# Two-layer graph attention on one core: x1 of layer 0 turned by DMA transposes of its 16-bit halves instead of by TensorE

## The chip, the cores and the metric

The kernel runs on one core of a Trainium2 chip. A core has TensorE (PE, matrix products and transposes through PSUM), VectorE (DVE), ScalarE (ACT), GpSimd (POOL) and SyncE (SP), whose queue issues every DMA of this kernel. The metric is the device time of one execution in microseconds, as a median over runs: 2969.35 before the change (3 runs, 2967.16 to 2970.29).

## The reference

`x` is 128 graphs of 64 nodes with 768 features, in f32; `adj` is a 0/1 matrix of each graph. Two layers follow each other, each with a residual and a layernorm. Cut to what is computed:

```python
# layer 0: additive graph attention, 12 heads of 64, a gate, residual, layernorm
h = einsum('bnd,ade->bane', x, W); th = tanh(h)
attn = th @ w_src + swap(th @ w_dst)              # one term of the row node, one of the column node
attn = where(attn >= 0, attn, 0.2 * attn)
attn = softmax(where(adj, attn, -999.0))
f = elu(einsum('banm,bame->bane', attn, h) + b)   # heads side by side
gate = sigmoid(x @ H_w.T + H_b)
x = layernorm(x + gate * f + (1 - gate) * x)      # the kernel's x1
# layer 1: scaled dot-product attention, 6 heads of 128, mask adj
q, k, v = heads(x @ Wq + bq), heads(x @ Wk + bk), heads(x @ Wv + bv)
ctx = softmax(q @ k.T / sqrt(128) + where(adj, 0, -9e15)) @ v
x = layernorm(x + ctx @ Wf + bf)
```

## The kernel before

**Tiles.** The 8192 nodes are 64 tiles of 128 rows (two graphs each), taken as 32 pairs of 256 rows (`PAIR`, `NP` = 32). A product of a pair with a 768x768 weight is cut into 2x2 blocks and done with seven block products instead of eight, by the scheme of Strassen and Winograd: sums of blocks of the data (`block_sums`, L184) and of the weight (`weight_sums`, L165) come first, and the results are added together on the way out of PSUM. A `Job` (L200 to L250) is one such product, and `step(job, i)` (L257) issues block product i (three matmuls of f32, which show as six in the trace) and then the way out of the step before it. The jobs have letters: `h` is x times W, `g` the gate, `v` the values of layer 1, `q` and `k` its queries and keys. Capital letters, and `u`, are jobs of a neighbouring turn: `H` is the `h` of the next pair, `u` the `v` that the turn before began.

**Turns.** Layer 0, with the `v` product of layer 1, is one loop of 33 turns (L875 to L978). Turn p computes `h` and the gate of pair p (its tiles are called n0 and n1) and finishes attention, elu, gate, residual and layernorm of pair q = p - 1 (tiles t0 and t1), turns its x1 and begins its `v`. The order of the block products in a turn is written out by hand: `FIRST` (turn 0), `SECOND` (turn 1), `TURN` without its first two steps (turn 2), `TURN` (turns 3 to 31), and `LAST` (turn 32, in which queries and keys of layer 1 begin). All other work hangs on positions in that list: `was(pos, ...)` for the old pair, `at(pos, ...)` for the new one. The actions of a position are emitted behind its block product, in each engine's own queue, which runs strictly in that order. Tables such as `LAST_AT` send a position elsewhere in some turns.

**What a turn of the old pair does.** `probs_by_nodes` transposes the probabilities, `attend` multiplies them with h, `features` divides by the sums and takes the exponential, `elu1` and `gated` make x1, `stats` and `normed` its layernorm (ScalarE writes x1, SP stores it to `x1_d` for layer 1's residual). `by_features` (L814) then brings a tile of x1 into the layout with features on partitions: two times three 128x128 transposes on TensorE into PSUM (`transposed`, L734), each three copied by ScalarE into `x1T`, which holds the pair. `x1T` is stored to `x1T_d` for queries and keys (`spill_features`), and is the data of the `v` job. `value_sums` (L855) allots four tiles `sv` and prepares their sums on VectorE.

**What it does for the new pair.** `products` (L656) takes tanh of h and multiplies it by both attention vectors, one on VectorE, one on GpSimd; `terms` (L665) sums per head into `sd`, stores the column term to DRAM (`dstd`) and loads it back broadcast to all rows (`dd`, two transfers); `with_bias` adds the bias to h and swaps halves of it through two transfers (`hx`); `logits`, `leaky`, `masked`, `exps` make the unnormalized probabilities. `x_sums` makes the block sums of the next pair's x on GpSimd.

**Queues.** Each `dma_start` is on SP, which executes them in the order of emission, and an instruction that waits holds all behind it. A tile of a pool with `bufs=1` (`x1T`, `sv`) can be written again only after its last reader.

The positions of the old code around the turning of x1:

```python
was(8, do(by_features, t1), do(stats, t0))
was(9, do(normed, t0))
was(12, do(v_begins))
was(15, lambda: v_sums[q][0](), lambda: v_sums[q][1](), do(spill_features, q))
was(16, lambda: v_sums[q][2]())
was(19, lambda: v_sums[q][3]())
...
was(11, do(by_features, t0))
```

Of the kernel before, what the change touches and what calls it, by code (L numbers as in the profile page):

```python
# [8 lines left out]

F32 = mybir.dt.float32  # L10
U8 = mybir.dt.uint8
AF = mybir.ActivationFunctionType
ALU = mybir.AluOpType
AX = mybir.AxisListType

P = 128
N = 64
D = 768
KC = D // P
HK = KC // 2  # L20
HALF = D // 2
H0, E0 = 12, 64
J0 = H0 // 2
EP = E0 + 2
H1, E1 = 6, 128
# [5 lines left out]
PAIR = 2  # L31
# [10 lines left out]
B11, B21, B22, T1, T2, T3, T4 = range(7)  # L42
# [21 lines left out]


LAST = [
    "u4", "u3", "q1", "q2", "k1", "k2", "q6", "q5", "q7", "Q1", "q4", "Q2", "q3", "k6", "k5", "k7",
    "Q6", "k4", "k3", "v1", "v2", "v6", "v5", "v7", "K1", "v4", "v3",
]
LAST_REST = [(1, 2), (0, 5), (1, 6), (0, 7), (1, 5), (1, 7), (0, 4), (0, 3), (1, 4), (1, 3)]  # L70
LAST_AT = {3: 3, 4: 4, 5: 6, 6: 8, 7: 9, 8: 11, 9: 12, 11: 15, 12: 16, 15: 20, 16: 20, 19: 22}

ENDS = [
    (0, 1), (0, 2), (0, 6), (0, 5), (0, 7), (1, 1), (0, 4), (0, 3), (1, 6), (1, 5),
    (1, 7), (1, 2), (1, 3), (1, 4),
]
TURN = [
    "h1", "h2", "u4", "u3", "h6", "g1", "h5", "h7", "g2", "g6", "h4",
    "h3", "g5", "g7", "v1", "v2", "g4", "v6", "g3", "v5", "v7",
]  # L80

THIRD_AT = {pos: max(pos - 2, 0) for pos in range(len(TURN))}
TURNS = {
    0: (FIRST, FIRST_AT, {}),
    1: (SECOND, SECOND_AT, SECOND_OLD),
    2: (TURN[2:], THIRD_AT, THIRD_AT),
}


# [1 line left out]
def kernel(  # L91
# [21 lines left out]
    nc = tc.nc  # L113
    NP = x.shape[0]
# [15 lines left out]

    x1_d = [dram.tile([P, PAIR, D], F32, name=f"x1d_{p}") for p in range(NP)]
    x1T_d = [dram.tile([P, KC, PAIR * P], F32, name=f"x1Td_{p}") for p in range(NP)]
    v_d = [dram.tile([P, D], F32, name=f"vd_{t}") for t in range(2 * NP)]
    dst_d = [dram.tile([P, H0], F32, name=f"dstd_{t}") for t in range(2 * NP)]

# [38 lines left out]
    def all_of(steps):  # L174
        for s in steps:
            s()

    def sum_tiles(pool, tag, n, name):
        return [
            pool.tile([P, HK, n], F32, tag=f"{tag}{i}", name=f"{tag}{i}_{name}", bufs=1)  # L180
            for i in range(1, 5)
        ]
# [345 lines left out]
    with ExitStack() as ph, ExitStack() as ph_r:  # L528
# [18 lines left out]
                ts.append(t)  # L547
            return ts

        def sums_of(eng, pool, tag, t, name):  # L550
            return block_sums(
                eng,
                sum_tiles(pool, tag, P, name),
                t[:, :HK, :P],
                t[:, HK:, :P],
                t[:, :HK, P:],
                t[:, HK:, P:],
            )
# [14 lines left out]
        wsd = sbr.tile([P, 2, D], F32, name="wsd", bufs=1)  # L573
        nc.sync.dma_start(out=wsd[:, 0, :], in_=wdst.partition_broadcast(P))
        nc.sync.dma_start(out=wsd[:, 1, :], in_=wsrc.partition_broadcast(P))
        A[0], x_steps = sums_of(G, sbr, "sx", xTs[0], "x0")
        all_of(x_steps)
        t1, t2, t4, t3 = weight_sums(V, w0_w)
        all_of((t1, t2, t3, t4))
# [2 lines left out]
        def work(name):  # L582
            return sb.tile([P, D], F32, tag="work", name=name, bufs=5)
# [59 lines left out]
        def v_job(p):  # L643
# [9 lines left out]
                lambda b: S.copy(at(1, 0), b),  # L653
            )

        def products(t):  # L656

            h = st[t]["h"]
            th = sbr.tile([P, 2, D], F32, tag="th", name=f"th_{t}")
            S.activation(th[:, 1, :].rearrange("p (a e) -> p a e", e=E0), h[:, :, :E0], AF.Tanh)  # L660
            V.tensor_tensor(th[:, 0, :], th[:, 1, :], wsd[:, 0, :], ALU.mult)  # L661
            G.tensor_tensor(th[:, 1, :], th[:, 1, :], wsd[:, 1, :], ALU.mult)  # L662
            st[t]["th"] = th

        def terms(t):  # L665

            th = st[t].pop("th")
            sd = small.tile([P, 2 * H0], F32, tag="sd", name=f"sd_{t}")
            V.tensor_reduce(sd, th.rearrange("p s (a e) -> p (s a) e", e=E0), AX.X, ALU.add)
            st[t]["sd"] = sd  # L670
            nc.sync.dma_start(out=dst_d[t], in_=sd[:, :H0])
            dd = work(f"dd_{t}")
            for g in range(2):
                nc.sync.dma_start(
                    out=dd[g * N : (g + 1) * N, :],
                    in_=dst_d[t][g * N : (g + 1) * N, :]
                    .rearrange("m a -> (m a)")
                    .partition_broadcast(N),
                )
            st[t]["dd"] = dd  # L680
# [128 lines left out]
            next(st[t].pop("norm"), None)  # L809
            nc.sync.dma_start(out=x1_d[t // 2][:, t % 2, :], in_=st[t]["x1"])  # L810

        x1Ts, B = {}, {}

        def by_features(t):  # L814
            p, i = divmod(t, 2)
            if p not in x1Ts:
                x1Ts[p] = sb.tile([P, KC, PAIR * P], F32, tag="x1T", name=f"x1T_{p}", bufs=1)
            x1 = st[t].pop("x1")
            for half in range(2):
                transposed(  # L820
                    x1Ts[p][:, 3 * half : 3 * half + 3, i * P : (i + 1) * P],
                    x1[:, half * HALF : (half + 1) * HALF],
                    f"x1Tp_{t}_{half}",
                )

        def spill_features(p):
            nc.sync.dma_start(out=x1T_d[p], in_=x1Ts[p])
# [25 lines left out]
                nc.sync.dma_start(out=v_d[t], in_=st[t].pop("v"))  # L853

        def value_sums(q):  # L855
            B[q], v_sums[q] = sums_of(V, sb, "sv", x1Ts[q], f"v{q}")

        def x_sums(p):
            operands, steps = sums_of(G, sbr, "sx", xTs[p], f"x{p}")
            all_of(steps)  # L860
            A.setdefault(p, {}).update(operands)

        def third_begins():
            x = xTs[2]
            A[2] = {1: x[:, :HK, :P], 2: x[:, HK:, :P]}
            jobs["H"] = h_job(2)

        row_sums = []

# [10 lines left out]
        for p in range(NP + 1):  # L880
# [2 lines left out]
            t0, t1, n0, n1 = 2 * q, 2 * q + 1, 2 * p, 2 * p + 1  # L883
            if new:
                jobs["G"] = jobs.get("g")
                jobs["h"], jobs["g"] = jobs["H"] if p == 2 else h_job(p), gate_job(p)
            plan = {}

            turn, of_new, of_old = TURNS.get(p, (TURN, {}, {})) if new else (LAST, {}, LAST_AT)

            def at(pos, ok, *acts, places=of_new):
                if ok:
                    plan.setdefault(places.get(pos, pos), []).extend(acts)

            def was(pos, *acts):
                at(pos, old, *acts, places=of_old)

            def do(f, *args):
                return lambda: f(*args)
# [6 lines left out]
            was(0, do(probs_by_nodes, t1))  # L906
            at(0, old, do(exps, t0), do(gate_tanh, t1), places={0: 6} if p == 1 else of_old)
            was(1, do(residual, t1))
            was(2, do(attend, t1), do(gate_tanh, t0))
            was(3, do(features, t1), do(probs_by_nodes, t0), do(residual, t0))  # L910
            was(4, do(elu1, t1), do(gated, t1))
            was(5, do(attend, t0), do(stats, t1))
            was(6, do(features, t0), do(normed, t1))
            was(7, do(elu1, t0), do(gated, t0))
            was(8, do(by_features, t1), do(stats, t0))
            was(9, do(normed, t0))
            was(12, do(v_begins))
            was(15, lambda: v_sums[q][0](), lambda: v_sums[q][1](), do(spill_features, q))
            was(16, lambda: v_sums[q][2]())
            was(19, lambda: v_sums[q][3]())  # L920

            at(0, p + 1 < NP, do(load_xT, p + 1))
            at(3, new, lambda: adjs.__setitem__(p, load_adj(sb, 2 * p, PAIR, f"adj_{p}")))
            at(6, new, do(mask, p))
            at(4, 0 <= p - 2 < NP, do(spill_values, p - 2))
            at(8, new, do(inputs, p))
            at(11, new, do(products, n1))
            was(11, do(by_features, t0))
            at(12, new, do(products, n0))
            at(13, new, do(terms, n1), do(with_bias, n1))  # L930
            at(14, new, do(terms, n0), do(with_bias, n0))
            at(15, new, do(plus_one, p))
            at(16, new, do(logits, n1))
            at(17, new, do(leaky, n1))
            at(17, p + 1 < NP, do(x_sums, p + 1), places={17: 12} if p == 0 else of_new)
            at(18, new, do(masked, n1), do(logits, n0))
            at(19, new, do(exps, n1), do(leaky, n0))
            at(20, new, do(masked, n0))

            if p == NP - 1:  # L940

                q_sums = weight_sums(G, w0_w)[:2] + weight_sums(V, w0_w)[2:]
                k_sums = weight_sums(G, hw_w)
                for pos, block in ((2, B11), (3, B21), (8, T3), (15, B22)):
                    at(pos, True, do(load_block, wq, w0_w, block))
                for pos, block in ((6, B11), (9, B21), (19, T3), (19, B22)):
                    at(pos, True, do(load_block, wk, hw_w, block))
                at(16, True, q_sums[0])
                at(18, True, queries_begin, q_sums[1])
                at(19, True, lambda: all_of(row_sums[:2]))  # L950
            if p == NP:
                flush()
                for act in plan.pop(0):
                    act()
                for pos, act in zip((1, 2, 2, 3, 4, 5, 7, 9), row_sums[2:] + q_sums[2:] + k_sums):
                    plan.setdefault(pos, []).append(act)
# [4 lines left out]
                    at(8, True, do(load_block, wv, wv_w, block))  # L961
                at(7, True, lambda: V.tensor_scalar(b01_bc, b01_bc, 1.0, None, ALU.add))
            if p == 1:
                at(14, True, third_begins, places={})
                for pos, act in zip((4, 5, 7, 8), weight_sums(V, wv_w)):
                    at(pos, True, act, places={})
            for pos, acts in carried.items():
# [119 lines left out]
```

## Time and profile before

| what | us |
|---|---|
| median of 3 runs | 2969.35 |
| the profiled execution | 2970.77 |
| its span, first to last instruction | 2969.0 |
| TensorE busy within the span | 2925.2 |
| matmuls that transpose x1 (x1Tp, 384) | 52.6 |
| matmuls that transpose probabilities (pTp, 384) | 57.6 |
| ScalarE copies x1T out of PSUM (128) | 55.0 |
| mean granted TensorE clock | 0.995 |

Median time from issue to landing, and the size of one transfer: `dd<-dstd` 192 KB, 3.4 us; `x1d<-x` 384 KB, 2.6 us; `vd<-v` 384 KB, 2.9 us; `hx<-h` 99 KB, 3.1 us; `dstd<-sd` 6 KB, 1.9 us; `x1Td<-x1T` 768 KB, 4.8 us.

How to read it: busy time of a group is the union of its instructions, so matmuls that overlap are counted once, while the mean duration of one is longer. A timeline line has the start, the time to the end of the last of the merged instructions, the engine (SPq is SP's queue of DMA issues), the line of the kernel, the operation, what it writes and reads, how many were merged, and in brackets the idle time of the engine before it with what ended it. A line of windows has the stretch, its length, then the busy time and the number of instructions of PE, weight loads, DVE, ACT and POOL, the granted clock, the share of the DMA engines and GB/s.

### The profile page before, as it was taken

Reading aid. Unit: us, or ns where it says so; the run is one execution under the profiler, and the core shown is the slowest. Engines: PE = TensorE matmul, PEld = TensorE weight load, DVE = VectorE, ACT = ScalarE, POOL = GpSimd, SP = SyncE. Lnnn points to the kernel's source line nnn. Section 1 sums busy time; section 2 is a strip of 40 time slices with the busy share of each in tenths; the row PEclk is TensorE's granted clock in tenths of the full one; section 3 lists DMA queues with packets and bytes.
Section 4 is the critical chain, followed back from the end, with each engine's and each line's share of the span. In section 5 each row is a group of like instructions: output and inputs, shape, how many; then the busy total and the mean of one; then the engine's idle time right before and its main releaser. Section 6 shows DMA issues by size and latency. Waiting matters only on the chain.

```text
span 2969.0 us, 45314 instructions
## 1 busy us (share of the span) xinstructions
PE 2925.2 (99%) x18048; PEld 2023.0 (68%) x18048; DVE 1796.9 (61%) x3017; ACT 1009.0 (34%) x1761; POOL 811.1 (27%) x650
## 2 busy tenths in 40 slices
PE   7999999999999999999999999999999999999999
PEld 4566666666666666666578777787777887777875
DVE  6878888788788878887844344333343443443345
ACT  2344344444443444444422222222222222222221
POOL 2434333333343333333422212211111212121121
PEclk9999999999999999999999999999999999999999
DMA  5333333334333333343532211222212222112221
GB/s 171 122 109 114 107 121 115 103 118 128 104 119 104 121 113 106 115 129 103 176 97 77 70 60 55 86 86 76 68 52 64 86 76 73 59 57 82 87 80 48
DMA packets 179681, 284.81 MB, mean 96 GB/s; under 512 B 46736, under 2 KB 113296, under 8 KB 179472
## 3 DMA queue, kind: packets, MB, share of 16 engines
q1 hardware_dynamic: 179472, 281.93, 29.1%
q8 instruction: 143, 2.34, 0.3%
q14 instruction: 66, 0.54, 0.1%
HBM read 167.81 MB, written 101.06 MB: 91 GB/s over the span
## 4 chain that ended last, share of the span: by engine, by line
PE 94%; DVE 3%; DMA 1%; ACT 1%; issue 0%; SPq 0%; POOLq 0%; POOL 0%; DVEq 0%; ACTq 0%
PE y_k L222 8%; PE y_o L222 8%; PE y_q L222 8%; PE y_v L222 8%; PE y_h L222 8%; PE y_g L222 8%; PE z_v L222 4%; PE z_o L222 4%; PE z_k L222 4%; PE z_h L222 4%; PE z_q L222 4%; PE z_g L222 4%; PE x_k L222 2%; PE x_o L222 2%; PE x_q L222 2%; PE x_h L222 2%
## 5 line engine op out<-in xcount | busy, mean ns | idle before, releaser
L789 POOL TENSOR_TENSOR x<-gate,x 128x768 f32<-128x768 f32 x64 | 117.4, 1835 | 323.8 <-ACT gate L840 309.0
L457 POOL TENSOR_TENSOR y<-y,bf_bc 128x768 f32<-128x768 f32 x64 | 115.3, 1832 | 311.4 <-DMA y<-x1d 311.4
L481 DVE TENSOR_TENSOR y<-y_o,y 128x384 f32<-128x384 f32 x128 | 71.4, 557 | 202.1 <-PE y_o L222 198.0
L339 DVE TENSOR_TENSOR kT<-z_k,kT 128x256 f32<-128x256 f32 x96 | 40.8, 425 | 239.3 <-PE z_k L222 136.1
L662 POOL TENSOR_TENSOR th<-th,wsd 128x768 f32<-128x768 f32 x64 | 117.2, 1832 | 182.5 <-DVE th L661 182.5
L274 POOL TENSOR_TENSOR rs_b<-ve_b,minus_half 128x1 f32<-128x1 f32 x64 | 35.1, 548 | 452.5 <-DVE ve_b L272 451.7
L192 POOL TENSOR_TENSOR sq_q<-a,a 128x768 f32<-128x768 f32 x16 | 29.2, 1828 | 432.8 <-PE y_o L222 286.9
L222 PE MATMUL y_h<-w_wq,xT 128*128 128x384 f32 x384 | 136.3, 492 | 8.6 <-DMA w_wq<-in_w_dram 7.9
L222 PE MATMUL y_k<-a,hw_wk 128*128 128x256 f32 x576 | 144.6, 387 | 0.0
L222 PE MATMUL y_q<-a,w_wq 128*128 128x256 f32 x576 | 140.9, 381 | 1.9 <-ACT qT L338 1.9
L222 PE MATMUL z_v<-wv,sv_v 128*128 128x384 f32 x384 | 138.9, 498 | 3.2 <-DVE v L652 3.2
L222 PE MATMUL y_q<-sq_q,w_wq 128*128 128x256 f32 x576 | 140.3, 380 | 0.9 <-ACT qT L338 0.9
L222 PE MATMUL y_h<-w_wq,sx_x 128*128 128x384 f32 x384 | 136.5, 492 | 4.2 <-ACT h L622 4.2
L222 PE MATMUL z_q<-sq_q,w_wq 128*128 128x256 f32 x576 | 140.1, 379 | 0.0
L222 PE MATMUL y_k<-sq_q,hw_wk 128*128 128x256 f32 x576 | 140.1, 379 | 0.0
L222 PE MATMUL z_k<-sq_q,hw_wk 128*128 128x256 f32 x576 | 140.0, 379 | 0.0
L338 ACT ACTIVATE qT<-y_q,bq_c 128x256 f32<-128x256 f32 x144 | 67.4, 469 | 213.2 <-PE y_q L222 213.2
L222 PE MATMUL y_v<-wv,sv_v 128*128 128x384 f32 x384 | 136.6, 492 | 3.0 <-DVE sv_v L193 3.0
L386 ACT ACTIVATE sc<-sc 128x512 f32<-128x512 f32 x48 | 30.2, 630 | 319.3 <-DVE sc L385 319.3
L222 PE MATMUL z_h<-w_wq,sx_x 128*128 128x384 f32 x384 | 137.6, 495 | 0.9 <-DVE w_wq L168 0.9
L222 PE MATMUL y_g<-hw_wk,sx_x 128*128 128x384 f32 x384 | 134.9, 488 | 2.4 <-DVE hw_wk L171 2.2
L222 PE MATMUL y_v<-wv,x1T 128*128 128x384 f32 x384 | 136.1, 491 | 1.2 <-ACT x1T L739 1.0
(171 smaller groups left out, 6678.1 us busy)
## 6 DMA issues: line engine op xcount, KB each, us to landing
x<-in_x_dram SPq DMA_DIRECT2D x64, 384.0 KB, 3.6
dd<-dstd SPq DMA_DIRECT2D x128, 192.0 KB, 3.4
x1d<-x SPq DMA_DIRECT2D x64, 384.0 KB, 2.6
x1Td<-x1T SPq DMA_DIRECT2D x32, 768.0 KB, 4.8
vd<-v SPq DMA_DIRECT2D x64, 384.0 KB, 2.9
a<-x1Td SPq DMA_DIRECT2D x64, 384.0 KB, 3.6
v<-vd SPq DMA_DIRECT2D x384, 64.0 KB, 2.3
y<-x1d SPq DMA_DIRECT2D x64, 384.0 KB, 4.1
```

The costliest lines, as they stand in the source:

```text
L192: lambda: e.tensor_tensor(s1, a21, a22, ALU.add),
L222: T.matmul(to[:, : self.n], lhsT, rhs, start=kc == 0 and not more, stop=kc == HK - 1, skip_group_check=more,)
L274: G.tensor_tensor(rstd, ve, minus_half, ALU.pow)
L338: lambda mn, bk_: S.activation(at(*mn), bk_, AF.Identity, bias=bias(mn[1])),
L339: lambda mn, bk_: V.tensor_tensor(at(*mn), bk_, at(*mn), ALU.add),
L386: S.activation(sc, sc, AF.Exp, scale=SCALE)
L457: G.tensor_tensor(y, y, pools["bf"], ALU.add)
L481: V.tensor_tensor(at(*mn), b, at(*mn), ALU.add)
L662: G.tensor_tensor(th[:, 1, :], th[:, 1, :], wsd[:, 1, :], ALU.mult)
L789: G.tensor_tensor(xp, st[t]["gate"], xp, ALU.mult)
```

## The change

For the pairs q = 2 to 30, `by_features` is no longer called. `apart` splits each word of x1 into its upper and lower 16 bits with strided copies: on ScalarE, and for one half of the odd tile on GpSimd. `send` stores the two halves of a tile as separate rows to a new DRAM buffer `halves_d`. `turned` issues six DMA transposes of two-byte elements for the pair, [512 rows, 128 columns] each, from DRAM into the memory of `sv`. `joined` puts the halves together as words of `x1T` with four strided ScalarE copies. The pairs 0, 1 and 31 (`by_pe`) keep the TensorE transposes.

The steps of a turn are re-ordered: `v` now begins with its products 1 and 2 in the last two positions of the turn, and its other five (`u6 u5 u7 u4 u3`) run in the next turn; the first two products of the next pair's `h` are done a turn earlier (`H1 H2`) from turn 2 on. `sv` is one tile for both uses, `tanh` and `spread` are split from `products` and `terms`, the sums of x are made in two parts, and the tables of positions are new.

```diff
 LAST = [
-    "u4", "u3", "q1", "q2", "k1", "k2", "q6", "q5", "q7", "Q1", "q4", "Q2", "q3", "k6", "k5", "k7",
-    "Q6", "k4", "k3", "v1", "v2", "v6", "v5", "v7", "K1", "v4", "v3",
+    "u6", "u5", "q1", "u7", "q2", "u4", "k1", "u3", "k2", "q6", "q5", "q7", "Q1", "q4", "Q2", "q3", "k6",
+    "k5", "k7", "Q6", "k4", "k3", "v1", "v2", "v6", "v5", "v7", "K1", "v4", "v3",
 ]
...
 TURN = [
-    "h1", "h2", "u4", "u3", "h6", "g1", "h5", "h7", "g2", "g6", "h4",
-    "h3", "g5", "g7", "v1", "v2", "g4", "v6", "g3", "v5", "v7",
+    "h6", "u6", "h5", "u5", "h7", "u7", "g1", "h4", "u4", "g2", "h3",
+    "u3", "g6", "g5", "g7", "H1", "H2", "g4", "g3", "v1", "v2",
 ]
 
-THIRD_AT = {pos: max(pos - 2, 0) for pos in range(len(TURN))}
+TURN_AT = {11: 8, 12: 13, 13: 12, 14: 14, 16: 15, 17: 16, 18: 17, 19: 18}
+THIRD = [
+    "h6", "u4", "h5", "u3", "h7", "g1", "h4", "g2", "h3", "g6", "g5", "g7",
+    "H1", "H2", "g4", "g3", "v1", "v2",
+]
...
+NO_NEXT = [
+    "h6", "u6", "h5", "u5", "h7", "u7", "g1", "h4", "g2", "u3", "h3",
+    "g6", "g5", "g7", "u4", "g4", "g3", "v1", "v2",
+]
...
+        def apart(t):
+
+            sp = work(f"sp_{t}").bitcast(U16).rearrange("p (two e) -> p two e", two=2)
+            x1 = words(st[t].pop("x1"))
+            if t % 2:
+                G.tensor_copy(sp[:, 0], x1[:, 0])
+            else:
+                S.copy(sp[:, 0], x1[:, 0])
+            S.copy(sp[:, 1], x1[:, 1])
+            st[t]["halves"] = sp
+
+        def send(t):
+            p, i = divmod(t, 2)
+            nc.sync.dma_start(
+                out=halves_d[p][:, i * P : (i + 1) * P, :].rearrange("h t d -> t h d"),
+                in_=st[t].pop("halves"),
+            )
+
+        def turned(p):
+
+            sv[p] = sb.tile([P, 4, HK, P], F32, tag="sv", name=f"sv_{p}", bufs=1)
+            for c in range(KC):
+                nc.sync.dma_start_transpose(
+                    out=landing(p)[:, c],
+                    in_=halves_d[p][:, :, c * P : (c + 1) * P].rearrange("h t f -> (h t) f"),
+                )
+
+        def landing(p):
+            return (
+                sv[p].rearrange("p s k t -> p (s k t)").bitcast(U16).rearrange("p (c ht) -> p c ht", c=KC)
+            )
+
+        def joined(p):
+            x1Ts[p] = sb.tile([P, KC, PAIR * P], F32, tag="x1T", name=f"x1T_{p}", bufs=1)
+            dst = x1Ts[p].bitcast(U16).rearrange("p c (t two) -> p two c t", two=2)
+            land = landing(p).rearrange("p c (two t) -> p two c t", two=2)
+            for kh in range(2):
+                for half in range(2):
+                    rows = slice(kh * HK, (kh + 1) * HK)
+                    S.copy(dst[:, half, rows], land[:, half, rows])
+
...
+            by_pe = q in (0, 1, NP - 1)
...
-            was(8, do(by_features, t1), do(stats, t0))
+            was(8, *[do(by_features, t1)] * by_pe, do(stats, t0))
             was(9, do(normed, t0))
-            was(12, do(v_begins))
-            was(15, lambda: v_sums[q][0](), lambda: v_sums[q][1](), do(spill_features, q))
-            was(16, lambda: v_sums[q][2]())
-            was(19, lambda: v_sums[q][3]())
+            if by_pe:
+                was(12, do(v_begins))
+                was(15, lambda: v_sums[q][0](), lambda: v_sums[q][1](), do(spill_features, q))
+                was(16, lambda: v_sums[q][2]())
+                was(19, lambda: v_sums[q][3]())
+            else:
+                was(7, do(apart, t1))
+                was(8, do(send, t1))
+                was(10, do(apart, t0))
+                was(17 if new and p < NP - 1 else 16, do(joined, q))
+                was(18 if p < NP - 1 else 17, do(v_begins))
+                was(18, lambda: v_sums[q][0](), lambda: v_sums[q][1](), do(spill_features, q))
+                was(19, lambda: v_sums[q][2]())
+                was(20, lambda: v_sums[q][3]())
...
-            at(4, 0 <= p - 2 < NP, do(spill_values, p - 2))
+            at(15 if p == NP - 1 else 13, 0 <= p - 2 < NP, do(spill_values, p - 2), places=of_old)
             at(8, new, do(inputs, p))
-            at(11, new, do(products, n1))
-            was(11, do(by_features, t0))
+            at(11, new, do(tanh, n1), do(products, n1))
+            was(11, *[do(by_features, t0)] * by_pe)
+            at(13, new, do(terms, n1))
...
+            if p >= 2:
+                at(11, new, do(tanh, n0), places=of_old)
+            else:
+                at(12, new, do(tanh, n0))
             at(12, new, do(products, n0))
-            at(13, new, do(terms, n1), do(with_bias, n1))
-            at(14, new, do(terms, n0), do(with_bias, n0))
+            if p >= 2 and new:
+                at(12, not by_pe, do(send, t0), places=of_old)
+                at(13, True, do(spread, n1), *[do(turned, q)] * (not by_pe), do(with_bias, n1), places=of_old)
+            at(14, new, do(terms, n0))
...
+                at(15, new, do(spread, n0), do(with_bias, n0), places=of_old)
```

## The prediction

> **What bounds the kernel now.** I read the busy shares first, then the slices, then single turns of layer 0 in the timelines.
>
> ```profile
> PE 2925.2 (99%) x18048; PEld 2023.0 (68%) x18048; DVE 1796.9 (61%) x3017; ACT 1009.0 (34%) x1761; POOL 811.1 (27%) x650
> ...
> PE   7999999999999999999999999999999999999999
> ...
> DVE  6878888788788878887844344333343443443345
> ```
>
> TensorE is busy throughout, and layer 0 (the first half) has VectorE at 0.8 besides: it is the second bound there. What a removed matmul is worth is therefore read from the start of one matmul group to the start of the next, not from the mean durations, which overlap. One turn, TensorE:
>
> ```profile
> 805.42 2.10 PE L222 MATMUL x_g<-hw_wk,xT 128*128 128x384 f32 x6
> 807.36 0.82 PE L738 MATMUL x1Tp<-ident,x 128*128 128x128 f32 x6
> 808.01 2.10 PE L222 MATMUL y_g<-hw_wk,sx_x 128*128 128x384 f32 x6
> 809.95 2.10 PE L222 MATMUL y_h<-w_wq,xT 128*128 128x384 f32 x6
> ...
> 852.96 0.82 PE L738 MATMUL x1Tp<-ident,x 128*128 128x128 f32 x6
> ```
>
> One block product takes 809.95 - 808.01 = 1.94 us; the six transposes of one tile take 808.01 - 807.36 = 0.65; a turn takes 852.96 - 807.36 = 45.60, without a gap. The same turn on the DMA queue of SP and on VectorE:
>
> ```profile
> 818.83 0.33 SPq L671 DMA_DIRECT2D dstd<-sd  x1
> 820.27 1.16 SPq L674 DMA_DIRECT2D dd<-dstd  x2
> 821.54 0.54 SPq L690 DMA_DIRECT2D hx<-h  x1
> 822.12 0.59 SPq L691 DMA_DIRECT2D hx<-h  x1
> 822.80 0.54 SPq L671 DMA_DIRECT2D dstd<-sd  x1
> 825.00 1.10 SPq L674 DMA_DIRECT2D dd<-dstd  x2
> ```
> ```profile
> 817.07 1.74 DVE L669 TENSOR_REDUCE sd<-th 128x24 f32<-128x1536 f32 x1
> ...
> 821.44 1.31 DVE L192 TENSOR_TENSOR sv_v<-x1T 128x384 f32<-128x384 f32 x1
> 822.78 1.24 DVE L193 TENSOR_TENSOR sv_v<-sv_v,x1T 128x384 f32<-128x384 f32 x1
> ...
> 831.34 1.52 DVE L698 TENSOR_TENSOR att<-dd,sd 128x768 f32<-128x768 f32 x1
> ```
>
> Here the second dd was issued at 825.00 and used at 831.34: the turn had some 2 us of slack behind a landing of 3.4 us. That slack is what the change spends.
>
> **What is removed.** Pairs 2 to 30 lose both by_features calls: 29 x 2 x 0.65 = 37.7 us of TensorE, 1.30 a turn. Pairs 0, 1 and 31 keep theirs. ScalarE loses four copies of 0.48 us a turn.
>
> **What is added off TensorE, a turn.** ScalarE gets three copies in apart and four in joined, each of 768 elements; the trace has no two-byte strided copy, and its rows of 768 elements are 0.84 to 1.03 us (gate, x). At 0.85 this is 7 x 0.85 - 1.93 = 4.0 us on an engine with 20.4 of 46 us busy: free, except where joined stands in a chain (below). At 1.03 joined alone is 0.7 longer. GpSimd's copy is bounded by its 384-element row (1.0) and its 768-element row (1.83); the transposes that read it come five products (9.7 us) later, and behind its send in SP's queue stand only x's loads, used as late: nothing. The sends are two more writes like x1d<-x (384 KB, landing 2.6 us).
>
> **The wait that the change adds.** All transfers go through SP in order. In the new order its queue reads: x1 of t0, dstd of n1, halves of t0, two vd, two dd of n1, six transposes, two hx of n1, dstd of n0, two dd of n0, two hx of n0. The transposes wait for the halves to land and for product u3, the last reader of sv. VectorE adds u3's result before it reduces sd of n1. So a loop closes once a turn: u3, sd, SP's queue, dd of n0, att of n0, the sums of v, u6 of the next turn, u3. From the start of u6 to the end of u3 TensorE needs, at rows of the timeline (steps of 1.94, one of 2.04 behind each attend, attend 0.96, a pT group 0.79), 24.2 us. A turn without stall is 45.60 - 1.30 = 44.30; so from the end of u3 to the next u6 there are 20.1 us. The chain, in us behind the end of u3:
>
> - add of u3 on VectorE 0.65, sd of n1 1.74: 2.4. Its dstd issues; halves and two vd follow (0.33 + 0.40 + 0.80 = 1.5), as long as the 1.44 from dstd to dd in the row above. Two dd: 3.95 to 5.1.
> - halves, issued at 2.75, land 2.6 later: 5.35, where the first transpose can go.
> - six issues of i each. No row shows a transpose; issues on SP take 0.32 (x1d<-x) to about 1.0 us (x<-in_x_dram, 2.01 for two; adj 0.96). So 1.9 to 6.0. I take 0.55, the dd and hx rows, which like it spread short pieces: 3.3, done at 8.65. hx of n1 also waits for GpSimd (th of n0 1.82, bias 1.67, done about 7.6); it comes in time. Two hx 1.13: 9.8.
> - dstd of n0, then 1.45 (n1's row) to 2.2 (n0's, 822.80 to 825.00): dd of n0 starts at 11.25 to 12.0, the second 0.58 later, and lands 3.4 behind: 15.2 to 16.0.
> - VectorE itself would be ready at 14.7: sd of n0 (7.6), two gates (8.7), att of n1 2.0, h 0.55, the wait for Prelu to 11.65, the masking 3.0. So it now waits 0.5 to 1.3.
> - att of n0 1.9, a gate 0.55, two sums 2.55: 20.2 to 21.0 against 20.1. The stall is 0.1 to 0.9; with 0.1 of semaphore hops I take 0.6.
>
> With i = 0.32 the queue is freed at 8.75 instead of 9.8, dd is in time, and nothing stalls. With i = 1.0 all is 2.7 later: a stall of 3.3.
>
> The second chain has the same root: att of n1 ends at 10.7, Prelu at 11.65, joined's first two copies at 13.35, and v1 may start at 7 x 1.94 = 13.55. It just fits, if the first three transposes have landed by 11.65 (5.35 + 3 x 0.55 + 2.6 = 9.6).
>
> **Rows and rules.** The transfer itself: 3072 rows of 256 bytes a pair; the trace's own packets of 256 bytes took 18 ns, of 64 bytes 11 ns. Over 16 engines that is 3.5 us, or 17 us if the pieces written are short (24,576 of 64 bytes). I take the former, hidden under the 3.3 us of issue, because rows are read whole. The Trainium skill speaks against the change: "VectorE: DVE Perf Modes", section "The three transpose paths", gives the DMA crossbar 1309 ns for a 128x128 block of 2-byte data and TensorE 390, and advises TensorE where PSUM will do; 24 such blocks one after the other would be 31 us a pair, a loss near 20 us a turn. The same skill, "DMA: Bandwidth & Descriptors", section "Latency and other measured facts", has 261 GB/s for transposing transfers, an estimate of 3.0 us a pair; no run so far shows either.
>
> **The moved steps.** Five of seven v products now run in the next turn, so the number of products is the same: nothing on TensorE. Turn 2, turn 31 and the last one are re-ordered; there TensorE idles now:
>
> ```profile
> 1450.00:1500.00 50.00, 42.52 (x236) 27.84 (x234) 44.26 (x46) 16.65 (x29) 30.04 (x14) 0.93 0.47 159
> 1500.00:1550.00 50.00, 48.14 (x287) 37.43 (x286) 17.61 (x33) 15.24 (x31) 4.76 (x3) 0.97 0.26 84
> ```
>
> The third column is TensorE's busy time: 7.5 + 1.9 = 9.3 us idle. At best the five products moved here fill it, at worst as much is lost; I take 0 of -9 to +9.
>
> **Sum.** 29 x (1.30 - 0.60) = 20.3 us. The profiled execution took 2970.8 (span 2969.0 and 1.8 around it): 2950.5. The median of the runs is 1.4 lower: 2949.
>
> **Rivals and chances.**
>
> 1. *Part of the gain* (stall 0 to 1.1 a turn): 2949, own range 2932 to 2963. Chance 0.38.
> 2. *All of it*: i near 0.35, dd in time. 29 x 1.30 = 37.7: 2932. For it: the two chains miss by tenths only. Against: VectorE has 38.5 of 44.3 us of work in its queue, summed from its rows. Chance 0.20.
> 3. *No change* (within 0.2%, 6 us, about what a measurement can tell from none): a stall of 1.1 to 1.5, i of 0.63 to 0.70. Chance 0.08.
> 4. *Slower, by SP's queue*: transposes issue slowly and hold dd of n0, so VectorE waits for att of n0 and TensorE for the v sums. It decides from i = 0.55 + 0.7 / 6 = 0.67. At 1.0: 29 x (3.3 - 1.3) = 58, 3027. For it: the slowest issues in the trace are that long, and dstd's landing would be queued behind the transposes. Against: most issues take 0.3 to 0.6. Chance 0.27.
> 5. *Slower, by the transfer*: short pieces, 17 us a pair. The last lands at 5.35 + 17 + 2.6 = 25, joined's second pair ends at 26.7, v2 may go at 15.5: 11 us a turn, less 1.3, times 29: 3250. Against: nothing in a turn with the DMA engines 0.35 busy shows such pieces at this volume. Chance 0.07.
>
> Faster is 1 and 2, 0.58; same 0.08; slower 0.34. For 8 in 10, the range goes from case 2 with most of the hand-over's gain (2926) to case 4 at i = 1.0 (3030); left out are case 5, a part of 4 and a little below.
>
> **What would show it.** A turn in steady state between 44.3 and 45.4 us; transposes issued at 0.3 to 0.65 us each, the last landing some 3 us later; VectorE waiting for dd of n0 by up to 1 us, or TensorE for sv at u6. It is wrong if a transpose takes SP over 0.67 us, if joined waits for a landing and v1 for joined, or if the turn's length is set by another loop than the one through u3.

## The result and the profile after

The changed kernel took 3105.48 us (3100.21 to 3110.06, 4 runs) against 2968.41 (2967.16 to 2970.29, 4 runs): 1.0461 times the time before, interval 1.0441 to 1.048. It is slower by 137 us. Here and below a ratio is taken against runs of the kernel before made beside that kernel, with a 95% interval and without the slow executions (two, both beside the first experiments). The forecast was 2949 and the range ended at 3030, so both missed, on the side of rival 4.

The profiled execution spans 3108.3 us, against 2969.0 before. Busy shares, slices and the chain that ended last, from the page of the kernel after:

```profile
PE 2935.2 (94%) x17700; PEld 2001.6 (64%) x17700; DVE 1759.0 (57%) x3017; ACT 1132.3 (36%) x1848; POOL 876.6 (28%) x679
...
PE   7998989999998989899979999999999999999999
...
DVE  6876767667677767776664333434333343433435
...
PE 66%; SPq 12%; DMA 8%; DVE 8%; issue 3%; ACT 3%; POOL 1%; POOLq 0%; DVEq 0%; ACTq 0%
```

TensorE no longer fills its slices in the first half, and VectorE fell with it: neither is the bound of layer 0 any more. SP's queue has 12% of the chain. The account of the 139.3 us between the spans: 37.7 us of transposes are gone, TensorE's idle time rose from 2969.0 - 2925.2 = 43.8 to 3108.3 - 2935.2 = 173.1 (+129.3), and the work that stayed took 2935.2 - (2925.2 - 37.7) = 47.7 longer. Where TensorE idles, in us in total, times and longest, from its waits after:

```profile
PE y_v L244 <- ACT pT L767: 65.4, 28, 3.7
PE y_v L244 <- ACT x1T L893: 44.2, 29, 5.8
PE x_v L244 <- ACT x1T L893: 20.4, 28, 1.7
```

Three places of a turn, 130.0 us in all: the whole rise of the idle time is there. The first is u6, the two others are v1 and v2, the first products that read x1T. Now one turn on SP's queue (start, duration, line, transfer, number of issues):

```profile
936.48 1.86 SPq L702 DMA_DIRECT2D dd<-dstd  x2
938.45 7.74 SPq L876 DMA_TRANSPOSE sv<-halvesd  x6
946.28 0.54 SPq L718 DMA_DIRECT2D hx<-h  x1
946.86 0.60 SPq L719 DMA_DIRECT2D hx<-h  x1
947.56 0.54 SPq L696 DMA_DIRECT2D dstd<-sd  x1
949.26 1.11 SPq L702 DMA_DIRECT2D dd<-dstd  x2
```

Six transposes hold the queue for 7.74 us, 1.29 each; issues of other kinds around them take 0.54 to 0.93. sd of n0 was ready long before its dstd could be issued, as the same turn on VectorE shows (in brackets: idle time before, and what ended it):

```profile
937.70 1.75 DVE L694 TENSOR_REDUCE sd<-th 128x24 f32<-128x1536 f32 x1 [1.92 <-POOL th L688]
...
941.49 2.79 DVE L726 TENSOR_TENSOR att<-dd,sd 128x768 f32<-128x768 f32 x1 [0.98 <-DMA dd<-dstd]
...
953.57 1.51 DVE L726 TENSOR_TENSOR att<-dd,sd 128x768 f32<-128x768 f32 x1 [5.31 <-DMA dd<-dstd]
...
956.04 0.56 DVE L215 TENSOR_TENSOR sv<-sv,x1T 128x384 f32<-128x384 f32 x1
```

sd ends at 939.45, its dstd starts at 947.56. VectorE then idles 5.31 us in front of att of n0, and the sums of v stand behind att. TensorE:

```profile
930.11 2.10 PE L244 MATMUL z_v<-wv,sv 128*128 128x384 f32 x6
...
947.06 2.20 PE L244 MATMUL y_v<-wv,x1T 128*128 128x384 f32 x6 [1.31 <-ACT x1T L893]
949.67 2.20 PE L244 MATMUL x_v<-wv,x1T 128*128 128x384 f32 x6 [0.40 <-ACT x1T L893]
...
956.70 2.17 PE L244 MATMUL y_v<-wv,sv 128*128 128x384 f32 x6 [2.24 <-ACT pT L767]
```

The last row is u6. The profile puts its wait down to pT on ScalarE, but u6 starts 0.1 us after the second v sum of VectorE ends (956.04 + 0.56): that is its releaser. From the u6 before, at 906.21, the turn takes 956.70 - 906.21 = 50.49 us instead of 45.60. The waits at v1 and v2 lie inside the same turn and did not set its length here: the loop through u3, the transposes, dd of n0 and u6 does not pass through them.

### The profile page after: what moved, and what is told of

It reads as the page before. It is cut to its first block, busy times and chain, and to the rows that moved or that the text cites. A ratio compares the mean times of both kernels' runs of the same rounds, so it can differ in the third digit from the quotient of the medians.

```text
span 3108.3 us, 44958 instructions
## 1 busy us (share of the span) xinstructions
PE 2935.2 (94%) x17700; PEld 2001.6 (64%) x17700; DVE 1759.0 (57%) x3017; ACT 1132.3 (36%) x1848; POOL 876.6 (28%) x679
## 4 chain that ended last, share of the span: by engine, by line
PE 66%; SPq 12%; DMA 8%; DVE 8%; issue 3%; ACT 3%; POOL 1%; POOLq 0%; DVEq 0%; ACTq 0%
PE y_o L244 8%; PE y_k L244 8%; PE y_q L244 8%; PE y_v L244 6%; SPq L876 5%; PE z_o L244 4%; PE z_k L244 4%; DMA x1Td<-x1T 4%; PE z_q L244 4%; PE y_h L244 3%; PE z_v L244 3%; PE z_h L244 3%; SPq L702 2%; PE y_g L244 2%; PE x_o L244 2%
## 5 line engine op out<-in xcount | busy, mean ns | idle before, releaser
L817 POOL TENSOR_TENSOR x<-gate,x 128x768 f32<-128x768 f32 x64 | 131.4, 2053 | 600.8 <-ACT gate L909 582.5
L726 DVE TENSOR_TENSOR att<-dd,sd 128x768 f32<-128x768 f32 x64 | 125.0, 1953 | 203.8 <-DMA dd<-dstd 203.8
L244 PE MATMUL y_v<-wv,sv 128*128 128x384 f32 x384 | 164.6, 574 | 70.9 <-ACT pT L767 65.4
L244 PEld LDWEIGHTS y_v<-wv,sv 128*128 128x128 f32 x384 | 80.8, 217 | 129.1 <-ACT pT L767 71.3
L694 DVE TENSOR_REDUCE sd<-th 128x24 f32<-128x1536 f32 x64 | 111.9, 1748 | 59.1 <-POOL th L688 59.1
L736 ACT ACTIVATE att<-att 128x768 f32<-128x768 f32 x64 | 53.9, 843 | 249.6 <-DVE att L726 249.4
L244 PEld LDWEIGHTS y_v<-wv,x1T 128*128 128x128 f32 x384 | 71.8, 194 | 106.7 <-ACT x1T L893 62.0
```

The lines of the kernel that those rows point to most:

```text
L244: T.matmul(to[:, : self.n], lhsT, rhs, start=kc == 0 and not more, stop=kc == HK - 1, skip_group_check=more,)
L726: V.tensor_tensor(att3, dd.rearrange("p (m a) -> p a m", a=H0), sd[:, H0:].unsqueeze(2).to_broadcast([P, H0, N]), ALU.add,)
L736: S.activation(att, att, AF.Prelu, alpha=LEAKY)
L817: G.tensor_tensor(xp, st[t]["gate"], xp, ALU.mult)
```

## The experiments

**The order alone.** All pairs but 30 are again turned by TensorE; the moved v products and the rest of the new order stay.

```
-            by_pe = q in (0, 1, NP - 1)
+            by_pe = q != NP - 2
```

> The new order of steps and the new positions, but x1 turned by TensorE in every pair except 30 (one pair of 32 goes through the DMA transposes). Theory (SP's queue: 7.7 us of transpose issues ahead of dd of n0): without the transposes the order alone costs little, 2955 to 2990 us. Rival (the order and the moved v products cost the time, whatever turns x1): it stays near 3100, at least 3060. If the order alone costs half, 3000 to 3060.

2966.92 us, ratio 0.9989 (0.9977 to 1.0001). The order by itself costs nothing; the whole loss comes with the new way of turning x1, its copies and its transfers.

**Plain loads in place of the transposes.** The same six issues at the same place of the queue, of the same rows; the transposition is left out.

```
-                nc.sync.dma_start_transpose(
-                    out=landing(p)[:, c],
-                    in_=halves_d[p][:, :, c * P : (c + 1) * P].rearrange("h t f -> (h t) f"),
+                nc.sync.dma_start(
+                    out=landing(p)[:, c].rearrange("p (a f) -> p a f", f=P),
+                    in_=halves_d[p][:, :, c * P : (c + 1) * P].rearrange(
+                        "h (a t) f -> t (h a) f", t=P
+                    ),
```

> The six DMA transposes of a pair become six plain DMAs that read the same 512 rows of 256 bytes each and write the same 128 KB into the same tile, without transposing: the transposition of x1 is left out for pairs 2 to 30, all waits and bytes stay. Theory (the issue time of a transpose on SP, 1.29 us, is the price): plain issues take 0.5 to 0.7 us, so dd of n0 goes out 3.6 to 4.7 us earlier a turn; 2940 to 2985 us. Rival (the bytes and short packets, or the ScalarE and GpSimd copies, are the price): 3080 to 3110.

2995.73 us, ratio 1.0086 (1.0056 to 1.0115). SP's queue of this kernel, and two of TensorE's waits:

```profile
916.44 3.73 SPq L876 DMA_DIRECT2D sv<-halvesd  x6
...
921.51 0.53 SPq L696 DMA_DIRECT2D dstd<-sd  x1
924.53 1.10 SPq L702 DMA_DIRECT2D dd<-dstd  x2
```
```profile
PE y_v L244 <- ACT x1T L895: 47.6, 29, 6.0
PE y_v L244 <- ACT pT L767: 4.1, 8, 0.9
```

At 3.73 / 6 = 0.62 us an issue, 110 of the 137 us are gone, though every copy and every byte is still there, and TensorE's wait at u6 falls from 65.4 to 4.1 us. But the time stays 26 us above before and over the expected band. Two things were missed: dstd of n0 now takes 924.53 - 921.51 = 3.0 us until dd can follow, where the changed kernel took 949.26 - 947.56 = 1.7 (the six transfers are still under way then; that they are the cause was not tested), and v1 waits here too (1.32 us in this turn, 47.6 in all). That second wait does not come from the issue price.

**dd of n0 by another queue.** dstd and dd of the even tiles are issued by ScalarE, so that they need not stand behind the transposes.

```
+        def by_act(t):
+            return nc.scalar if t % 2 == 0 and 6 <= t else nc.sync
...
-            nc.sync.dma_start(out=dst_d[t], in_=sd[:, :H0])
+            by_act(t).dma_start(out=dst_d[t], in_=sd[:, :H0])
...
-                nc.sync.dma_start(
+                by_act(t).dma_start(
```

> The store of dstd and the two loads of dd of tile n0 are issued from ScalarE's queue instead of SP's from pair 3 on, so they no longer stand behind the transposes; the transposes are as they were. Theory (dd of n0 held in SP's queue sets the turn): the 5.3 us wait of VectorE for dd goes, the wait of TensorE at u6 goes and with it the half clock; what is left are the waits for joined at v1 and v2 (1.3 + 0.5 us a turn, against 1.3 gained): 2960 to 3010 us. Rival (dd is late because the DMA engines are full with the transposes): VectorE waits for dd as before and the time stays over 3080.

3051.27 us, ratio 1.0273 (1.0243 to 1.0302): better than the change by 54 us, and a miss of the expected band. VectorE's waits for dd fell from 203.8 to 42.9 us; a new wait took their place. ScalarE's timeline and TensorE's row behind it:

```profile
942.88 0.84 ACT L680 ACTIVATE th<-h 128x768 f32<-128x768 f32 x1
950.13 0.33 ACTq L699 DMA_DIRECT2D dstd<-sd  x1
953.04 1.12 ACTq L705 DMA_DIRECT2D dd<-dstd  x2
954.20 1.58 ACT L921 ACTIVATE x<-x 128x768 f32<-128x768 f32 x2 [10.48 <-issue]
...
958.79 3.89 PE L244 MATMUL y_v<-wv,x1T 128*128 128x384 f32 x6 [2.40 <-ACT x1T L896]
```

Between 943.7 and 954.2 ScalarE does no work: its queue stands at dstd until sd is there, then at dd until dstd has landed, 2.9 us later. Prelu (the activation of `leaky`) and joined are queued behind, and v1 behind joined.

**Twelve transposes of half the size.** 256 rows each instead of 512, the same bytes.

```
+                for h in range(2):
+                    nc.sync.dma_start_transpose(
+                        out=landing(p)[:, c, h * 2 * P : (h + 1) * 2 * P],
+                        in_=halves_d[p][h, :, c * P : (c + 1) * P],
+                    )
```

> Twelve transposes of 256 rows instead of six of 512 a pair, the same bytes. If the issue time of a transpose goes with its rows (0.65 us each), the time stays near 3105 (3090 to 3130). If each instruction has a fixed price of 1.29 us, SP is held 7.7 us longer a turn and the loop through dd of n0 grows by as much: 29 x 7.7 = 224, 3300 to 3350 us. In between, the share of both can be read from the issue row.

3296.19 us, ratio 1.1097 (1.1065 to 1.1129), 4 us under the band of the fixed price.

```profile
916.46 15.32 SPq L877 DMA_TRANSPOSE sv<-halvesd  x12
```

15.32 / 12 = 1.28 us each with half the rows: at 256 and 512 rows the price is one of the instruction, not of the bytes. Fewer and larger ones should then help.

**One transpose, and two.** The spill is laid out as [12 blocks, 256 tokens, 128 features], so that one instruction can take all 3072 rows, or two can take 1536 each.

```
-    halves_d = [dram.tile([2, PAIR * P, D], U16, name=f"halvesd_{p}") for p in range(NP)]
+    halves_d = [dram.tile([2 * KC, PAIR * P, P], U16, name=f"halvesd_{p}") for p in range(NP)]
...
-            for c in range(KC):
+            for c in range(0, 2 * KC, 12):
...
-                    in_=halves_d[p][:, :, c * P : (c + 1) * P].rearrange("h t f -> (h t) f"),
+                    in_=halves_d[p][c : c + 12].rearrange("hc t f -> (hc t) f"),
```

> One DMA transpose of 3072 rows a pair instead of six of 512: the halves lie in DRAM as [half and column block, row, 128], so the send writes pieces of 256 bytes and the six transposes become one, of the same bytes. Theory (each transpose has a fixed price of 1.28 us on SP, whatever its rows: six of 512 rows took 7.74, twelve of 256 took 15.3): SP is held 1.3 to 2 us, dd of n0 goes out 5.8 us earlier, the loop through it is shorter than TensorE's turn, and the removed transposes of TensorE show: 2930 to 2950 us. Rival (the DMA engines or the descriptors need the time, not the issue): the one transpose holds SP or lands as late as the six, joined waits and v1 with it, 3050 or more.

> The same layout with two transposes of 1536 rows a pair. Theory: SP is held 2.6 us, 1.3 more than with one; the chain through dd of n0 still fits, 2930 to 2955 us, within 10 us of the single one. Rival as there: 3050 or more.

One: 3038.86 us, ratio 1.0229 (1.0213 to 1.0244). Two (step and width 6 in place of 12): 3000.44, ratio 1.0102 (1.0085 to 1.0119). Both miss their bands. SP's queue and TensorE of the first, then SP's queue and VectorE of the second:

```profile
946.97 4.66 SPq L876 DMA_TRANSPOSE sv<-halvesd  x1
```
```profile
956.65 3.62 PE L244 MATMUL y_v<-wv,x1T 128*128 128x384 f32 x6 [3.15 <-ACT x1T L893]
```
```profile
920.70 3.77 SPq L876 DMA_TRANSPOSE sv<-halvesd  x2
```
```profile
924.08 1.69 DVE L726 TENSOR_TENSOR att<-dd,sd 128x768 f32<-128x768 f32 x1 [2.08 <-DMA dd<-dstd]
...
932.73 1.52 DVE L726 TENSOR_TENSOR att<-dd,sd 128x768 f32<-128x768 f32 x1 [2.98 <-DMA dd<-dstd]
```

Above some size the price grows: the median is 1.26 us for 512 rows, 1.95 for 1536 and 4.42 for 3072. The single transpose lands 6.7 us behind its issue in the median, and in the turn shown joined waits for it and v1 3.15 us for joined: that is the mechanism of its rival, though the time is 11 us under the rival's bound. Two gain 105 us over six, yet VectorE still waits for dd twice in a turn, in front of att of n1 as well, which stands ahead of the transposes in the queue. So the place in the queue may cost something too.

**The same two transposes in another order.** The halves of x1 are grouped by block of features in DRAM, so that either transpose feeds one pair of joined's copies. send of t0 moves ahead of dstd of n1, the two vd and the two hx to the end; the queue reads: halves of t0, dstd n1, two dd n1, first transpose, dstd n0, second transpose, two dd n0, four hx, two vd. The lines of the edit that set the order:

```
-                at(12, not by_pe, do(send, t0), places=of_old)
-                at(13, True, do(spread, n1), *[do(turned, q)] * (not by_pe), do(with_bias, n1), places=of_old)
+                at(11, not by_pe, do(send, t0), places=of_old)
+                at(13, True, do(spread, n1), *[do(turned, q, 0)] * (not by_pe), do(with_bias, n1), places=of_old)
...
-                at(15, new, do(spread, n0), do(with_bias, n0), places=of_old)
+                at(14, new and not by_pe, do(turned, q, 1), places=of_old)
+                at(15, new, do(spread, n0), do(crossed, n1), do(with_bias, n0), do(crossed, n0), places=of_old)
+                at(15, 2 < p < NP - 1, do(spill_values, p - 2), places=of_old)
```

(crossed issues hx, which with_bias did.)

> Two transposes of 1536 rows, cut by block of features so that joined can begin after the first; and SP's queue of pairs 3 to 30 in another order: halves of t0, dstd of n1, two dd of n1, first transpose, dstd of n0, second transpose, two dd of n0, then the hx and vd that stood ahead. Theory (what is late is what stands behind the transposes and the vd in SP's queue): from the two-transpose run, dd of n1 goes out about 1 us earlier, dd of n0 lands 3 to 4 us earlier, the first transpose lands 2 us earlier; the waits of VectorE for dd, of TensorE at v1 (1.33 us) and at u6 (0.6) go, and the removed 1.3 us a turn shows: 2930 to 2955 us, faster than both kernels. Rival (the DMA engines deliver late because all the transfers stand close together, whatever the order in the queue): within 15 us of the two-transpose run, 2985 to 3015.

2932.55 us (2930.89 to 2934.1, 4 runs) against 2968.53, ratio 0.9877 (0.9861 to 0.9894): 1.2% less than before, and less than the changed kernel by 173 us. Page, SP's queue, VectorE and TensorE of this kernel:

```profile
PE 2881.8 (98%) x17700; PEld 1988.2 (68%) x17700; DVE 1767.2 (60%) x3017; ACT 1136.3 (39%) x1848; POOL 892.7 (30%) x679
```
```profile
925.85 1.68 SPq L702 DMA_DIRECT2D dd<-dstd  x2
927.63 1.42 SPq L880 DMA_TRANSPOSE sv<-halvesd  x1
929.15 0.52 SPq L696 DMA_DIRECT2D dstd<-sd  x1
929.73 1.53 SPq L880 DMA_TRANSPOSE sv<-halvesd  x1
932.09 1.11 SPq L702 DMA_DIRECT2D dd<-dstd  x2
```
```profile
936.47 2.00 DVE L729 TENSOR_TENSOR att<-dd,sd 128x768 f32<-128x768 f32 x1 [0.17 <-DMA dd<-dstd]
```
```profile
902.45 2.20 PE L244 MATMUL z_v<-wv,sv 128*128 128x384 f32 x6
...
919.75 2.10 PE L244 MATMUL z_v<-wv,sv 128*128 128x384 f32 x6
...
935.23 2.10 PE L244 MATMUL y_v<-wv,x1T 128*128 128x384 f32 x6
937.17 2.10 PE L244 MATMUL x_v<-wv,x1T 128*128 128x384 f32 x6
...
946.52 2.20 PE L244 MATMUL z_v<-wv,sv 128*128 128x384 f32 x6
```

The second z_v is u3, which ends at 921.69. dd of n0 is issued 10.4 us behind it, where the changed kernel took 17.2 (the table below). VectorE waits 0.17 us for it, v1 and v2 start without a wait, and the turn, from the first z_v to the same product at 946.52, takes 44.07 us. The span is 36.7 below before: 37.7 of transposes removed, 5.7 less busy time in the rest, 6.7 more idle time; where the last two come from was not traced. The new order moves the send, the transposes, hx and vd at once; which of these moves counts was not taken apart.

**Order and number apart.** Three more kernels take the two edits one at a time: the six transposes behind dd of n0 and nothing else moved; the new queue order with six transposes, three at each place; the new layout with two transposes in the changed kernel's order. The edit of the first:

```
-                at(13, True, do(spread, n1), *[do(turned, q)] * (not by_pe), do(with_bias, n1), places=of_old)
+                at(13, True, do(spread, n1), *[do(turned, q)] * (not by_pe and p == NP - 1), do(with_bias, n1), places=of_old)
...
-                at(15, new, do(spread, n0), do(with_bias, n0), places=of_old)
+                at(15, new, do(spread, n0), *[do(turned, q)] * (not by_pe and p < NP - 1), do(with_bias, n0), places=of_old)
```

> The changed kernel with its six transposes issued behind the two dd of n0 instead of ahead of dstd of n0 (pairs 2 to 29). Theory (the price of 7.7 us sits in SP's queue and is only moved): dd of n0 is in time, but the third transpose lands about 17 us behind the end of u3 and the sixth about 21; with joined behind them v1 and v2 stall for some 7 us a turn: 3110 to 3170, no better than the changed kernel. Rival (only dd of n0 matters, the transposes have room to be late): below 3000.

> The queue order of the fast version with the changed kernel's own six transposes of 512 rows (three at the place of the first, three at the place of the second): the number of transposes is the only difference in the queue. Theory (both count: 7.7 us of fixed price on SP and what stands beside it): SP is held 4.8 us longer than with two, the transposes end 4 to 5 us later, dd of n0 some 4 us later; joined's second pair and dd of n0 are 2 to 3 us late: 2985 to 3040. Rival (the order alone was the fault): 2930 to 2960.

> The layout and the two transposes of the fast version, in the changed kernel's queue order. Theory: dd of both tiles still stands behind the vd or the transposes, as in the two-transpose run; only joined may begin earlier: 2980 to 3000. Rival (the cut by block of features makes the difference): 2930 to 2960.

Behind dd of n0: 3163.52 us, ratio 1.0657 (1.0636 to 1.0678). The dd waits are gone (43.5 us left), and joined is late in their place; TensorE of this kernel:

```profile
925.02 3.96 PE L244 MATMUL y_v<-wv,x1T 128*128 128x384 f32 x6 [6.11 <-ACT x1T L893]
```

So 7.74 us of issue fits on neither side of dd of n0. The other two, beside the two kernels already shown:

| | changed kernel's order | new order |
|---|---|---|
| six transposes | 3105.48 | 2996.36, ratio 1.0092 (1.0062 to 1.0121) |
| two transposes | 2999.53, ratio 1.0102 (1.0073 to 1.0132) | 2932.55 |

Number and order are worth 106 and 109 us alone and 173 together. The number changes together with the layout of `halves_d`, in which a send lands 3.6 us behind its issue instead of 2.8. Alone each takes most of the wait at u6 (65.4 us; 15.4 are left with two, none is listed in the new order) and leaves one at v1 or v2. From TensorE's waits, two transposes in the changed kernel's order and then six in the new one:

```profile
PE y_v L244 <- ACT x1T L894: 47.3, 29, 6.1
```
```profile
PE x_v L244 <- ACT x1T L897: 46.6, 29, 2.9
```

In the new order with six, v2 and att of n0 wait; SP's queue, VectorE and TensorE:

```profile
920.20 3.73 SPq L880 DMA_TRANSPOSE sv<-halvesd  x3
```
```profile
928.42 1.52 DVE L729 TENSOR_TENSOR att<-dd,sd 128x768 f32<-128x768 f32 x1 [3.23 <-DMA dd<-dstd]
```
```profile
927.52 2.20 PE L244 MATMUL x_v<-wv,x1T 128*128 128x384 f32 x6 [1.29 <-ACT x1T L897]
```

## Why the prediction was wrong

The step that failed is the third of the loop: "six issues of i each ... I take 0.55, the dd and hx rows", with bounds 0.32 and 1.0. It measured 1.29, outside both bounds. Nothing in the trace of before shows a transpose, and the choice was the row whose pieces looked alike; its upper bound came from issues of another kind and was no bound. The deciding point was i = 0.67. The prediction's formula at 1.29 gives a stall of 0.6 + 6 x 0.74 = 5.0 and 2970.8 + 29 x (5.0 - 1.3) = 3078 for the profiled execution, which took 3110.1. Rival 4's mechanism, SP's queue in front of dd of n0, is thus the right one and its price the term that was mis-sized, and the plain loads put 110 us on the price of its six issues (with the reservation that the loads land 4.0 us behind their issue in the median, the transposes 2.8).

The steps of the loop, in us behind the end of u3 (932.05 in the turn shown: 930.11 and a step of 1.94):

| step | forecast | measured |
|---|---|---|
| sd of n1 ends | 2.4 | 2.4 |
| dd of n1, both issued | 3.95 to 5.1 | 4.4 to 6.3 |
| first transpose issued | 5.35 | 6.4 |
| transposes issued | 8.65 | 14.1 |
| att of n1 ends | 10.7 | 12.2 |
| joined's first two copies end, v1 | 13.35, 13.55 | 14.95, 15.0 |
| dd of n0 issued | 11.25 to 12.0 | 17.2 |
| att of n0 starts | 15.2 to 16.0 | 21.5 |
| u6 of the next turn | 20.2 to 21.0 | 24.65 |

**The second chain** "just fits" in the forecast by 0.2 us and did not. It misses before any transpose is issued: the two dd of n1 took 1.86 us to issue instead of 1.15, behind the halves and the two vd, and att of n1 took 2.79 us instead of 2.0, after a wait. v1 waits 1.31 us in the changed kernel's turn, 1.32 with six plain loads and 1.33 with two transposes, whatever i is. With the plain loads these waits are 47.6 us, the larger part of the 64 us between 2995.7 and the 2932.55 of the reordered kernel, which keeps 8.2 of them. The new order sends dd of n1 ahead of the vd, and v1 no longer waits; giving each half of joined its own transpose did not do it alone, since v1 still waits 47.3 us with that cut in the old order. The prediction kept no range for this chain. v2 waits for another reason, which the prediction had only among its signs of being wrong: joined's second pair waits 0.66 us in the turn shown for the last transposes to land.

**A term was missing.** The work that stayed took 47.7 us longer. In the windows of the kernel after around the u6 at 906.21 (window, length, busy time and number of PE, PEld, DVE, ACT, POOL, then the granted clock, DMA share, GB/s):

```profile
906.00:909.00 3.00, 2.79 (x6) 1.62 (x7) 2.96 (x6) 0.21 (x1) 0.00 (x0) 0.72 0.56 194
909.00:912.00 3.00, 3.00 (x11) 1.45 (x10) 1.90 (x3) 1.45 (x2) 0.00 (x0) 0.71 0.00 0
912.00:915.00 3.00, 3.00 (x57) 2.09 (x57) 1.41 (x4) 2.29 (x5) 1.81 (x1) 1.00 0.00 0
```

The clock is down behind this wait: 6 us at a mean of 0.715 are 1.7 us lost, as 3.4 us at half clock would be. It does not go down behind each one. The next u6, at 956.70, waited longer, 2.24 us, and its window reads:

```profile
956.00:959.00 3.00, 2.30 (x7) 1.44 (x8) 2.95 (x6) 0.70 (x2) 0.00 (x0) 1.00 0.62 221
```

The turn from 906.21 took 50.49 us; the one before it, from a u6 at 857.50 whose clock stayed at 1.00 behind a wait of 2.23 us, took 48.71, which is 1.8 less. Over the span the mean clock is 0.985 against 0.995, which is 46.6 - 14.8 = 32 us. The rest, 16 us, fits the restarts: a group behind a wait shows 2.1 to 2.2 us where the step in a gapless row is 1.94; that part is argued, not shown. So a stall can cost more than its length. That 3078 + 32 = 3110 meets the measured time is luck in part: the idle time is 16 us below the formula's (129 us against 29 x 5.0 = 145), and the 16 us beyond the clock make up for it.

**Right as forecast.** The removal: the kernel with two reordered transposes gains 36.7 us of span, near the 37.7 of rival 2. The order of the moved products at nothing: 0.9989. ScalarE's copies, 0.83 us in apart and in joined 0.97 from one to the next, 1.04 from start to end (forecast 0.85, or 1.03), and GpSimd's at 0.82 (forecast 1.0 to 1.83): none of them sets a turn of 44.07 us. The transfer: 89,216 packets of 256 bytes against 128 before, at a median of 18 ns, so the rows are read whole and rival 5 falls. (Its 17 us rested on 24,576 pieces of 64 bytes; a pair's 3072 x 256 bytes make 12,288 of them, 8.4 us by the same sum.) The hand-over lies within its -9 to +9: all idle time that the reordered kernel has more than before is 6.7 us.

**The rules that were weighed.** The Trainium skill, "VectorE: DVE Perf Modes", section "The three transpose paths", would have made it 31 us a pair. One instruction here turns four such blocks in 1.29 us of issue, and the six of a pair are issued within 7.74 us: the estimate was four times the price found. Its advice for TensorE, which stands under "Rules for kernel authors" of the same page, held against the change as it was made, not against the reordered kernel with two transposes, which is 1.2% faster than the kernel before. The same skill, "Advanced Engine Details and Errata", section "X-Bar Transpose (TRN2)", has transposing DMAs as fast as regular ones. For the landing the traces show nothing against it (2.8 us behind the issue in the median, 4.0 for the plain loads of the same rows); for the issue they do not agree (1.29 against 0.62 for a plain load), and it was the issue that decided.

## What to carry to other kernels

When an operation moves to a DMA queue that others share, count first what its issue costs that queue and who stands behind it; if no row shows that price, the end of the range must stand well above the dearest issue seen. Put the short transfers that an engine waits for ahead of the long issues, and merge the long ones, but measure how far: here two of 1536 rows did better than six of 512 and than one of 3072. Two chains that fit by tenths of a microsecond are not two chances of a full gain but two places for a loss, and a wait of TensorE may cost a stretch at a lower clock besides its length.

## What the runs showed that was not expected

- A transposing DMA holds its queue for 1.24 us at 256 rows of 256 bytes, 1.26 at 512, 1.41 or 1.95 at 1536 and 4.42 at 3072 (medians). The two figures at 1536 go with the place in the queue: 1.95 where the two stand back to back, with the words in either grouping, and 1.41 where a dstd stands between them. One of 3072 is longer than two of 1536 together; why was not tried.
- Moving dstd and the two dd of a tile to ScalarE's queue stopped ScalarE for 10.5 us in the turn shown, since the wait for the landing stands in front of its arithmetic.
- TensorE's clock went down behind some waits at u6 and not behind others of the same length: behind 2.08 us at 906.21, not behind 2.23 at 857.50 or 2.24 at 956.70, all with shorter waits at v1 and v2 ahead of them (1.31 and 0.40 before the last). What decides between them is open. The Trainium skill, "TensorE: Matmul & The Clock Gate", section "What's actually happening", names an idle window of about 3.4 us for this; the stretch at the lower clock agrees with that length, the single wait ahead of it was shorter.
